# Attention masks of a two-layer graph network: transposed on TensorE, or by a casting DMA and a transposing DMA; with a sixth row buffer and a changed order of two small products

## The chip, the cores and the metric

The kernel runs on one core of a Trainium2 chip. The core has five engines, each with an instruction list of its own that it works through in order: TensorE (PE, with its weight loads shown apart as PEld), VectorE (DVE), ScalarE (ACT), GpSimd (POOL) and SyncE (SP). Engines wait for one another through semaphores. DMAs are issued here by SP and by POOL, in the order of those engines' lists. The metric is the time of one execution on the device in microseconds (us), the median of several runs; less is better.

## The reference, cut to what matters

The input x is 32 batches of 512 nodes with 256 features; adj is one 512 x 512 matrix of zeros and ones in int32 for each batch, about 3% of them ones. Two layers follow one another, and both read the same adj.

```
# layer 0
x = x + graph_conv(layernorm(x), adj)      # mean over neighbours, relu
x = x + ffn(layernorm(x))                  # tropical part and gated classical part

# layer 1, attention (4 heads of 64)
h      = einsum('bnd,hde->bhne', layernorm(x), W)
weight = leaky_relu(e_src[..., :, None] + e_dst[..., None, :])     # where adj == 1
weight = where(adj == 0, -1e9, weight)
att    = softmax(weight, axis=-1)
x      = x + layernorm_per_head(relu(att @ h + bias) + h)

# layer 1, mixer (8 heads of 64 slices)
sw = softmax((layernorm(x) @ W_x.T) @ W_slice.T / temp, axis=-1)   # nodes to 64 slices
st = sw.T @ fx / (sw.sum + 1e-5)                                   # slice tokens
ot = hydra(st)                # a scan over the 64 slice tokens, in both directions
x  = x + (sw @ ot) @ out_w.T + out_b
```

The attention types run from 1 to 5, but adj holds only 0 and 1, so one type counts. What the change touches is the mask `adj == 1` of the attention, which the kernel needs transposed: with the neighbour on the partitions and the node on the free axis.

## The kernel before, in words

**The two layers.** `layer0_sorted` does layer 0 for all batches. It sorts rows and gathers lines of a table, so it uses the DMA engines much. It ends at about 2324 us of the trace and leaves x in DRAM in a sorted order (`x2s`), with `ranks` saying where each row went. `layer1_plain` does layer 1. It is a generator: its constants and first preparations are woven into the last part of layer 0, up to its `yield True` at L1117. Both layers watch whether their shortcuts hold for the data; the findings are collected in `over`, and if any is set a plain version of both layers runs afterwards. With this input none is.

**Layer 1 by batch.** `attentions()` drives three generators a batch: `prepare(b)`, `attention(b)` and `norm(b)`.

- `prepare(b)` (L1156) gathers the batch's rows x on POOL with four indirect DMAs (L1162), normalises them (`normed`: statistics L1134 on VectorE, the power -0.5 at L30 and L31 on POOL, the scaling L1141 on ScalarE), adds a constant row by an accumulating DMA on POOL (`add_rows`, L949), and transposes the result (x3T, L1150 and L1151). It then forms h and both score vectors in one product (hp, L1188), their exponentials (L1191 to L1193) and a copy of h (ht, L1194). POOL adds a bias into hv (L1197); VectorE scales hv at L1210. The scores of the own node are transposed (minep, L1201), copied (L1203), written to DRAM by SP (ownd, L1205) and read back four times, once a head, as rows spread over all partitions (own, L1208). Tile own has 5 buffers.
- `attention(b)` (L1224) makes the weights of a head and of 128 neighbours in one VectorE instruction, att = max(own, other) * mask (`weigh`, L1221), 16 a batch. TensorE multiplies them with hv (avp, L1258) and sums them (adp, L1263).
- `norm(b)` (L1291 to L1313) adds ht, takes mean and mean square (the squares are written over ht at L1305, and reduced at L1307), and adds the normed values to x.

`mixer(g)` works on a group of GB = 2 batches: `slices` (layernorm, x4T, lgp L1344, exponentials sw L1345, the softmax over slices L1346 to L1351, yTp L1356, swp L1361), `tokens`, `scan` (the hydra part; `segp` L1500 are two products, one for each batch of the group, from the operands seg[0] and seg[1], and decay at L1502 is their exponential), and `unslice` (outp L1576, the addition to x L1578, the store of the result).

**The masks.** `masks(b)` is a generator that `prepare(b)` runs. For each of a batch's four tiles of 128 rows of adj it loads 256 KB of int32 (ai, L1087, issued by SP), turns it into bf16 on ScalarE (a, L1101), squares it on ScalarE (L1102), transposes its four blocks of 128 x 128 on TensorE into PSUM (maskp, L1092) and casts the result to uint8 on VectorE (mask, L1093; two buffers). ScalarE's two passes also leave row sums in `edges`. A sum of a that differs from the sum of its squares tells of values other than 0 and 1, and a sum of 0 of a node without a neighbour. Those become flags at L1610 to L1613. Batch 0's mask is made ahead, within layer 0.

**What sets the order.** Every tile name has a number of buffers, and an instruction that writes a buffer waits for the last reader of the one before. The program text is written in one order, by generators: `mixer` yields how many steps of preparation it wants, and the driver lets `attentions()` take them.

```python
PACE = 1.04 * GB * (TURNS + STEPS) / WANTED
for g in range(B // GB):
    for want in mixer(g):
        credit += want * PACE
        while credit >= 1.0:
            credit -= 1.0
            if next(ahead, True):
                credit = 0.0
```

STEPS counts the yields of a `prepare`. From this text a planner, with a cost for each instruction, fixes each engine's list before anything runs; a call within `keep_in_program_order` keeps its place in the text. A gather of batch b waits until the result of batch b - AHEAD_X is in the text (AHEAD_X = 5 buffers of x), so preparation runs at most so many batches ahead of `unslice`.

Of the kernel before, what the change touches and what calls it, by code (L numbers as in the profile page):

```python
# [864 lines left out]
def layer1_plain(tc, ident, eps, x2s, ranks, adj, w, out, over, ps):  # L865
# [21 lines left out]
    HE = HO + 1  # L887
    AP = AH // 2
    TURNS = AP * NT + 6
    STEPS = 15  # L890
    WANTED = 68
    AHEAD = 3
    ATT = 2 * (AHEAD + 2) + AP + 1
    HW = P // AH
    AHEAD_X = 2 * GB + 1
    PACE = 1.04 * GB * (TURNS + STEPS) / WANTED

    SMALL = 30.0 * 30.0 / D
# [2 lines left out]
    with ExitStack() as ctx:  # L901
# [3 lines left out]
        def ctile(name, shape):  # L905
            return cst.tile(shape, F32, tag=name, name=name)
# [8 lines left out]

        ones = ctile("ones", [P, P])
        nc.gpsimd.memset(ones, 1.0)
        identb = cst.tile([P, P], BF16, tag="identb", name="identb")
        nc.vector.tensor_copy(identb, ident)

        wa = ctile("wa", [P, DC, AH * HO + 2 * AH])
        for c in range(DC):
# [24 lines left out]
        def add_rows(xt, i):  # L947

            nc.gpsimd.dma_start(xt.rearrange("p t d -> p (t d)"), added[i].partition_broadcast(P), accum_op=ALU.add)  # L949

        yield
        edges = ctile("edges", [P, 2, B * NT])
        abias = const("abias", [P, AH * HO], w["gnn_bias"].rearrange("h e -> (h e)").partition_broadcast(P))
        gamma = const("gamma", [P, AH * HO], w["ln_gamma"].rearrange("h e -> (h e)").partition_broadcast(P))
        bfx = const("bfx", [P, KC, 1], w["b_fx"].rearrange("(k p o) -> p k o", p=P, o=1))
# [120 lines left out]
            nc.scalar.activation(ebsl, ebsl, AF.Exp)  # L1076

        se = ctx.enter_context(tc.tile_pool(name="e1", bufs=2, side="right", reuse_waits="tile"))
        masked = {}

        def masks(b, bank="any"):

            a, raw = [], []

            def load(t):
                raw.append(se.tile([P, N], I32, tag="ai", name=f"ai{b}_{t}", bufs=2))
                nc.sync.dma_start(raw[t], adj[b, t * P : (t + 1) * P, :])  # L1087

            def turn(t):
                pt = ps.tile([P, NT, P], BF16, tag=bank, name=f"maskp{b}_{t}")  # L1090
                for j in range(NT):
                    nc.tensor.transpose(pt[:, j, :], a[t][:, j * P : (j + 1) * P], identb)  # L1092
                nc.vector.tensor_copy(mask[:, :, t * P : (t + 1) * P], pt)  # L1093

            load(0)
            load(1)
            yield
            for t in range(NT):
                n = b * NT + t
                a.append(se.tile([P, N], BF16, tag="a", name=f"a{b}_{t}", bufs=3))  # L1100
                nc.scalar.activation(a[t], raw[t], AF.Identity, accum_out=edges[:, 0, n : n + 1])  # L1101
                nc.scalar.activation(raw[t], raw[t], AF.Square, accum_out=edges[:, 1, n : n + 1])  # L1102
                if t + 2 < NT:
                    load(t + 2)
                if t == 1:
                    mask = se.tile([P, NT, N], mybir.dt.uint8, tag="mask", name=f"mask{b}")
                    yield
                if t > 1:
                    turn(t - 2)
                    yield  # L1110
            for t in range(NT - 2, NT):
                turn(t)
                yield
            masked[b] = mask

        yield from masks(0, "mm")
        yield True  # L1117
        ps = ctx.enter_context(tc.tile_pool(name="p1", bufs=4, space=PSUM, reuse_waits="tile"))
        sb = ctx.enter_context(tc.tile_pool(name="s1", bufs=2, reuse_waits="tile"))
# [9 lines left out]
        def normed(xt, xn, name):  # L1129

            mv = sb.tile([P, NT, 2], F32, tag="mv" + name[0], name=f"mv{name}")
            for t in range(NT):
                st = sb.tile([P, 6], F32, tag="st" + name[0], name=f"st{name}_{t}", bufs=4)
                nc.vector.bn_stats(st, xt[:, t, :])  # L1134
                nc.vector.bn_aggr(mv[:, t, :], st)
            rs = sb.tile([P, NT], F32, tag="rs" + name[0], name=f"rs{name}")
            deviation(nc, rs, mv[:, :, 1], eps)
            shift = sb.tile([P, NT], F32, tag="shift" + name[0], name=f"shift{name}")
            nc.vector.scalar_tensor_tensor(shift, mv[:, :, 0], -1.0, rs, ALU.mult, ALU.mult)
            for t in range(NT):  # L1140
                nc.scalar.activation(xn[:, t, :], xt[:, t, :], AF.Identity, bias=shift[:, t : t + 1],  # L1141
                                     scale=rs[:, t : t + 1])
# [13 lines left out]
        def prepare(b):  # L1156

            while b >= AHEAD_X and b - AHEAD_X not in stored:
                yield True
            xt = xs[b] = sb.tile([P, NT, D], F32, tag="x", name=f"x{b}", bufs=AHEAD_X)  # L1160
            for t in range(NT):
                nc.gpsimd.indirect_dma_start(  # L1162
                    out=xt[:, t, :], out_offset=None, in_=x2s[b // SEG],
                    in_offset=bass.IndirectOffsetOnAxis(
                        ap=ranks[:, b * NT + t : b * NT + t + 1].bitcast(U32), axis=0))

            hv = sb.tile([P, NT, AH, HE], F32, tag="hv", name=f"hv{b}")
            xn = hv.rearrange("p t h e -> p (t h e)")[:, : NT * D].rearrange("p (t d) -> p t d", t=NT)
            edged = masks(b) if b not in masked else range(3)
            for i, _ in enumerate(edged):  # L1170
                if i < 3 or b not in masked:
                    yield
                if i == 2:
                    normed(xt, xn, f"c{b}")
                    add_rows(xt, 0)
                    yield
            mask = masked.pop(b)
            xnT = yield from turned(xn, "x3T", f"x3T{b}")
            yield


            ht = sb.tile([P, NT, AH * HO], F32, tag="ht", name=f"ht{b}")
            other = sb.tile([P, NT, AH], F32, tag="other", name=f"other{b}")
            mine = sb.tile([P, AH, NT], F32, tag="mine", name=f"mine{b}")
            for t in range(NT):
                ph = psum("any", f"hp{b}_{t}")
                for c in range(DC):
                    nc.tensor.matmul(ph[:, : AH * (HO + 2)], xnT[:, c, t * P : (t + 1) * P], wa[:, c, :],  # L1188
                                     start=c == 0, stop=c == DC - 1)
                d = ph[:, AH * HO : AH * HO + AH]  # L1190
                nc.scalar.activation(mine[:, :, t], ph[:, AH * (HO + 1) : AH * (HO + 2)], AF.Exp, scale=1.0 - SLOPE)  # L1191
                nc.scalar.activation(hv[:, t, :, HO], d, AF.Exp)
                nc.scalar.activation(other[:, t, :], d, AF.Exp, scale=SLOPE - 1.0)  # L1193
                nc.scalar.copy(ht[:, t, :], ph[:, : AH * HO])  # L1194
                yield

            nc.gpsimd.tensor_add(hv[:, :, :, :HO], ht.rearrange("p t (h e) -> p t h e", h=AH),  # L1197
                                 abias.rearrange("p (h e) -> p h e", h=AH).unsqueeze(1).to_broadcast([P, NT, AH, HO]))
            yield
            pt = psum("any", f"minep{b}")  # L1200
            nc.tensor.transpose(pt[: AH * NT, :P], mine.rearrange("p h t -> p (h t)"), ident)  # L1201
            row = sb.tile([AH * NT, P], F32, tag="turned", name=f"turned{b}", bufs=1)
            nc.scalar.copy(row, pt[: AH * NT, :P])  # L1203
            own_row = dr.tile([AH, N], F32, tag="own", name=f"ownd{b}")
            nc.sync.dma_start(own_row.rearrange("h (t p) -> (h t) p", p=P), row)  # L1205
            own = [wide("own", f"own{b}_{h}", AH + 1) for h in range(AH)]
            for h in range(AH):
                nc.sync.dma_start(own[h], own_row[h].partition_broadcast(P))  # L1208
            for t in range(NT):
                nc.vector.tensor_mul(hv[:, t, :, :HO], hv[:, t, :, :HO], hv[:, t, :, HO:].to_broadcast([P, AH, HO]))  # L1210
            ready[b] = mask, ht, hv, other, own
            yield
# [11 lines left out]
        def attention(b):  # L1224
# [52 lines left out]
            dt = back(dT, "dp")  # L1277
            rs = sb.tile([P, NT, AH], F32, tag="rs", name=f"rs{b}")
            nc.vector.tensor_scalar_max(rs, dt.rearrange("p (t h e) -> p t h e", t=NT, h=AH)[:, :, :, 0], 1e-30)
            nc.vector.reciprocal(rs, rs)  # L1280
            for q in range(AP):
                bt = back(vT[q], f"bp{q}_")
# [109 lines left out]
        def scan(g, uT):  # L1392
# [103 lines left out]
                    nc.tensor.matmul(pg[j * G : (j + 1) * G, i * G : (i + 1) * G], bcT[:, 0, j, :],  # L1496
                                     cpad[:, j, 2 * i : 2 * i + G], start=True, stop=True)
            pl = psum("any", f"segp{g}")
            for j in range(GB):
                nc.tensor.matmul(pl[j * G : (j + 1) * G, :], seg_l, seg[j], start=True, stop=True)  # L1500
            decay = inner(f"decay{g}")
            nc.scalar.activation(decay, pl, AF.Exp)  # L1502
# [104 lines left out]


        flags = over[:, 2 * AH + 3 :]
        nc.vector.tensor_sub(flags, edges[:, 1, :], edges[:, 0, :])  # L1610
        nc.vector.tensor_scalar(flags, flags, 0.0, None, ALU.not_equal)
        nc.vector.tensor_scalar(edges[:, 0, :], edges[:, 0, :], 0.5, None, ALU.is_lt)
        nc.vector.tensor_add(flags, flags, edges[:, 0, :])  # L1613


def layer1(tc, ident, eps, x2, adj, w, out):
# [632 lines left out]
```

## Time and profile before

| | |
|---|---|
| median of 3 runs | 4320.41 us (4319.69, 4320.41 and 4325.92) |
| the profiled execution | 4319.15 us |
| its span, first to last instruction | 4317.4 us |
| mean granted TensorE clock | 0.957 of full speed |
| busy: PE, PEld | 3852.3 us (89%), 2446.7 us (57%) |
| busy: DVE, ACT, POOL | 3233.1 us (75%), 2290.3 us (53%), 1540.2 us (36%) |
| moved by DMAs | 524.16 MB, 121 GB/s in the mean |
| 0 to 2200 us, mostly layer 0 | PE busy 1887 us, DMA engines 56% |
| 2324 to 2400 us, from layer 0 to layer 1 | PE busy 54 of 76 us |
| 2400 to 4180 us, layer 1 | PE busy 1683 us, DVE 1325, ACT 913, POOL 444, DMA engines 26% |

The page of the profile cuts the span into 40 equal slices and gives each engine's busy share in them in tenths. The groups of instructions name a line of the code, the engine, the operation, and what it writes and reads; then the busy time of all together, the mean of one in ns, and how long the engine stood idle just before them, with what ended the idle time. Waits are listed by the instruction that waited and the one that released it. The timeline lists single instructions with their start and their length in us, and in brackets the idle time before. SPq is SP's queue: the length there is the time to issue a DMA, not to carry it out; its landing is given apart.

### The profile page before, as it was taken

Reading aid. Unit: us, or ns where it says so; the run is one execution under the profiler, and the core shown is the slowest. Engines: PE = TensorE matmul, PEld = TensorE weight load, DVE = VectorE, ACT = ScalarE, POOL = GpSimd, SP = SyncE. Lnnn points to the kernel's source line nnn. Section 1 sums busy time; section 2 is a strip of 40 time slices with the busy share of each in tenths; the row PEclk is TensorE's granted clock in tenths of the full one; section 3 lists DMA queues with packets and bytes.
Section 4 is the critical chain, followed back from the end, with each engine's and each line's share of the span. In section 5 each row is a group of like instructions: output and inputs, shape, how many; then the busy total and the mean of one; then the engine's idle time right before and its main releaser. Section 6 shows DMA issues by size and latency. Waiting matters only on the chain.

```text
span 4317.4 us, 57903 instructions
## 1 busy us (share of the span) xinstructions
PE 3852.3 (89%) x20311; PEld 2446.7 (57%) x20311; DVE 3233.1 (75%) x7008; ACT 2290.3 (53%) x4756; POOL 1540.2 (36%) x1940
## 2 busy tenths in 40 slices
PE   5567998899999999889998899999999999999997
PEld 4454565566655665555555355565555555565555
DVE  6668877888788977877775777767777777778763
ACT  3344655556655656556664455545554455555432
POOL 2355643664435644354332222222222222222210
PEclk8678999999999999999999999999999999999998
DMA  4557654665546654386542322222222232222210
GB/s 130 161 160 228 191 162 133 192 214 168 149 127 218 197 165 136 109 279 192 153 128 69 78 67 71 79 62 67 74 69 69 76 79 76 75 69 74 62 30 16
DMA packets 260811, 524.16 MB, mean 121 GB/s; under 512 B 39800, under 2 KB 131588, under 8 KB 260509
## 3 DMA queue, kind: packets, MB, share of 16 engines
q0 software_dynamic: 124800, 366.28, 29.5%
q1 hardware_dynamic: 135708, 154.08, 11.4%
q8 instruction: 162, 2.65, 0.3%
q14 instruction: 141, 1.15, 0.1%
HBM read 463.11 MB, written 57.17 MB: 121 GB/s over the span
## 4 chain that ended last, share of the span: by engine, by line
PE 35%; DVE 26%; DMA 10%; issue 9%; POOL 8%; ACT 5%; SPq 0%; POOLq 0%; DVEq 0%; ACTq 0%
PE clsp L623 5%; DVE att L1221 4%; PE gatep L623 4%; PE po L652 3%; PE avp L1258 3%; DVE acc L637 3%; DMA rows<-table,xs 2%; PE yTp L1356 2%; DVE best L599 2%; DMA best<-table,xs 2%; DVE sw L1351 2%; DMA rows<-table,tops 2%; DVE sst L1349 2%; DVE sw L1346 2%; PE oTp L1544 1%
## 5 line engine op out<-in xcount | busy, mean ns | idle before, releaser
L623 PE MATMUL clsp<-xnT,wc 128*128 128x512 f32 x1024 | 522.4, 629 | 47.2 <-ACT cls L625 40.3
L623 PE MATMUL gatep<-xnT,wg 128*128 128x512 f32 x1024 | 496.8, 604 | 9.4 <-ACT gate L625 7.4
L652 PE MATMUL po<-wd,acc 128*128 128x256 f32 x2048 | 451.7, 380 | 5.2 <-DVE acc L641 4.3
L652 PEld LDWEIGHTS po<-wd,acc 128*128 128x128 f32 x2048 | 386.8, 190 | 70.7 <-issue 9.1
L1221 DVE SCALAR_TENSOR_TENSOR att<-own,other,mask 128x512 f32<-128x512 f32 x512 | 365.7, 743 | 78.5 <-DMA own<-ownd 78.5
L599 DVE SCALAR_TENSOR_TENSOR best<-rows,xs,best 128x1024 f32<-128x1024 f32 x212 | 271.0, 1280 | 132.6 <-ACT best L593 74.9
L637 DVE SCALAR_TENSOR_TENSOR acc<-past,fld,acc 128x512 f32<-128x512 f32 x448 | 332.1, 744 | 32.5 <-ACT past L636 24.3
L623 PEld LDWEIGHTS gatep<-xnT,wg 128*128 128x128 f32 x1024 | 196.1, 196 | 249.9 <-issue 198.4
L632 ACT ACTIVATE acc<-tz,fld 128x512 f32<-128x512 f32 x256 | 199.0, 777 | 260.1 <-PE tz L630 235.2
L636 ACT ACTIVATE past<-tz,fld 128x512 f32<-128x512 f32 x448 | 291.3, 693 | 73.3 <-DVE acc L637 72.7
L596 POOL DMA_INDIRECT rows<-table,xs x212 | 252.9, 1193 | 188.6 <-DVE best L599 124.8
L623 PEld LDWEIGHTS clsp<-xnT,wc 128*128 128x128 f32 x1024 | 183.7, 200 | 184.6 <-issue 113.3
L435 PE MATMUL pm<-h,adj 128*128 128x258 f32 (+1 forms) x1024 | 182.3, 325 | 98.5 <-DVE keep L428 35.7
L1258 PE MATMUL avp<-att,hv 128*32 128x512 f32 x2048 | 254.9, 603 | 13.9 <-DVE att L1221 13.8
L625 ACT ACTIVATE gate<-gatep,fld 128x512 f32<-128x512 f32 x256 | 175.5, 685 | 158.3 <-PE gatep L623 129.2
L1344 PE MATMUL lgp<-wsl,x4T 128*128 128x512 f32 x512 | 243.0, 613 | 16.6 <-ACT sw L1345 7.2
L1356 PE MATMUL yTp<-sw,x 128*128 128x512 f32 x512 | 237.8, 602 | 18.9 <-DVE sw L1351 18.2
L554 POOL DMA_INDIRECT xs<-rows_of,order x128 | 155.0, 1211 | 266.8 <-DVE acc L637 104.3
L1162 POOL DMA_INDIRECT x<-x2s,ranks x128 | 136.5, 1066 | 297.7 <-DVE att L1221 133.3
L1309 POOL TENSOR_TENSOR mu<-mu,eps 128x16 f32<-128x16 f32 x32 | 111.2, 3475 | 348.1 <-DVE mu L1308 347.9
L1576 PE MATMUL outp<-v,swT 128*128 128x256 f32 x1024 | 227.6, 381 | 0.0
L435 PEld LDWEIGHTS pm<-h,adj 128*128 128x128 f32 x1024 | 152.5, 214 | 123.9 <-issue 73.0
(590 smaller groups left out, 8643.8 us busy)
## 6 DMA issues: line engine op xcount, KB each, us to landing
adj<-in_adj POOLq DMA_DIRECT2D x128, 256.0 KB, 5.6
ai<-in_adj SPq DMA_DIRECT2D x128, 256.0 KB, 2.8
x<-added POOLq DMA_DIRECT2D x64, 512.0 KB, 5.2
own<-ownd SPq DMA_DIRECT2D x128, 256.0 KB, 3.6
rows_of<-keep SPq DMA_DIRECT2D x32, 550.0 KB, 4.3
x<-in_x SPq DMA_DIRECT2D x32, 512.0 KB, 6.6
xs<-bd POOLq DMA_DIRECT2D x32, 512.0 KB, 5.7
x2s<-xs SPq DMA_DIRECT2D x32, 512.0 KB, 3.0
```

Source lines behind the costliest of these rows:

```text
L435: nc.tensor.matmul(pm[:, : c1 - c0], a[:, i, t * P : (t + 1) * P], h[:, i, c0:c1], start=i + c0 == 0, stop=i + 1 == NT and c0 > 0)
L596: nc.gpsimd.indirect_dma_start(out=row, out_offset=None, in_=table, in_offset=bass.IndirectOffsetOnAxis(ap=idxs[:, k : k + 1].bitcast(U32) ...
L599: nc.vector.scalar_tensor_tensor(m, row, vals[:, k : k + 1], m, ALU.add, ALU.max)
L623: nc.tensor.matmul(pf, wf[:, c, f * P : (f + 1) * P], xnT[:, c, :], start=c == 0, stop=c == DC - 1)
L636: nc.scalar.activation(r, z, AF.Relu, bias=fld[:, f, AT + b : AT + b + 1])
L637: nc.vector.scalar_tensor_tensor(y, r, fld[:, f, CH + b : CH + b + 1], y, ALU.mult, ALU.add)
L652: nc.tensor.matmul(po[:, i, :], acc[f][:, t * P : (t + 1) * P], wd[:, f, :], start=f == 0, stop=f == FC - 1)
L1221: nc.vector.scalar_tensor_tensor(e, own[h], other[:, j, h : h + 1], mask[:, j, :], ALU.max, ALU.mult)
L1258: nc.tensor.matmul(pv[p][k * HW : (k + 1) * HW, :], hv[:, j, h, e : e + HW], weighed[b, h, j], **ends)
L1344: nc.tensor.matmul(pf, xnT[:, c, t * P : (t + 1) * P], wsl[:, c, :], start=c == 0, stop=c == DC - 1)
L1356: nc.tensor.matmul(py, xn[:, t, c * P : (c + 1) * P], sw[:, t, :], start=t == 0, stop=t == NT - 1)
L1576: nc.tensor.matmul(po[:, :D], swT[:, k, t * P : (t + 1) * P], v[:, k, :], start=k == 0, stop=k == KC - 1)
```

## The change

**Masks.** `masks()` goes, and with it the bf16 identity `identb`. Two small functions take its place. `shorten(b)` has POOL copy the whole adj[b] from DRAM to DRAM as bf16, one casting DMA (L1085 of the changed kernel; the tile short has three buffers, and the call keeps its place in the order of the text). `turn(b)` has SP load it with one transposing DMA of 512 KB into the mask (L1091), which is now bf16 with two buffers. Batches 0 and 1 are shortened ahead, within layer 0, and batch 0's mask is loaded there. `prepare(b)` starts by issuing turn(b) and shorten(b + 2), behind the row gathers. It yields the same number of times up to the normalisation as it did with a ready mask, so STEPS goes from 15 to 12.

**Watching the data.** One ScalarE pass over the whole mask, (mask - 0.5) squared, takes the place of two passes a tile. It writes into ht as scratch, before ht is made, and leaves a sum in `edges`; with zeros and ones alone the sum over a row of 2048 is 0.25 * 2048. Whether a node has a neighbour is now asked of the attention's denominator dt, a comparison of 128 x 4 values on VectorE. The flags at the end follow.

**A sixth buffer.** AHEAD_X goes from 5 to 6: x has six buffers, and a gather may come a batch earlier.

**decay's products.** The two products of segp are issued in the opposite order, seg[1] first, the operand that is made last.

```diff
-    STEPS = 15
+    STEPS = 12
-    AHEAD_X = 2 * GB + 1
+    AHEAD_X = 2 * GB + 2
...
-        identb = cst.tile([P, P], BF16, tag="identb", name="identb")
-        nc.vector.tensor_copy(identb, ident)
...
-        edges = ctile("edges", [P, 2, B * NT])
+        edges = ctile("edges", [P, B + B * NT])
+        centre = ctile("centre", [P, 1])
+        nc.gpsimd.memset(centre, -0.5)
...
-        def masks(b, bank="any"):
...
-        yield from masks(0, "mm")
+        short, masked = {}, {}
+        def shorten(b):
+            if b < B:
+                short[b] = dr.tile([N, N], BF16, tag="short", name=f"short{b}", bufs=3)
+                tc.keep_in_program_order(nc.gpsimd.dma_start(short[b], adj[b], max_dma_last_dim=8192))
+        def turn(b):
+            if b < B:
+                masked[b] = se.tile([P, NT, N], BF16, tag="mask", name=f"mask{b}")
+                nc.sync.dma_start_transpose(masked[b], short.pop(b))
+        for b in range(2):
+            shorten(b)
+            yield
+        turn(0)
         yield True
...
-            edged = masks(b) if b not in masked else range(3)
-            for i, _ in enumerate(edged):
-                if i < 3 or b not in masked:
-                    yield
-                if i == 2:
-                    normed(xt, xn, f"c{b}")
-                    add_rows(xt, 0)
-                    yield
+            if b:
+                turn(b)
+            shorten(b + 2)
+            yield
+            yield
+            yield
+            normed(xt, xn, f"c{b}")
+            add_rows(xt, 0)
+            yield
             mask = masked.pop(b)
...
             ht = sb.tile([P, NT, AH * HO], F32, tag="ht", name=f"ht{b}")
+            nc.scalar.activation(ht.rearrange("p t e -> p (t e)").bitcast(BF16), mask.rearrange("p t n -> p (t n)"),
+                                 AF.Square, bias=centre, accum_out=edges[:, b : b + 1])
...
+            nc.vector.tensor_scalar(edges[:, B + b * NT : B + (b + 1) * NT],
+                                    dt.rearrange("p (t e) -> p t e", t=NT)[:, :, 0], 0.0, None, ALU.is_le)
...
-            for j in range(GB):
+            for j in reversed(range(GB)):
                 nc.tensor.matmul(pl[j * G : (j + 1) * G, :], seg_l, seg[j], start=True, stop=True)
...
-        nc.vector.tensor_sub(flags, edges[:, 1, :], edges[:, 0, :])
-        nc.vector.tensor_scalar(flags, flags, 0.0, None, ALU.not_equal)
-        nc.vector.tensor_scalar(edges[:, 0, :], edges[:, 0, :], 0.5, None, ALU.is_lt)
-        nc.vector.tensor_add(flags, flags, edges[:, 0, :])
+        nc.vector.tensor_copy(flags, edges[:, B:])
+        nc.vector.scalar_tensor_tensor(flags[:, :B], edges[:, :B], 0.25 * NT * N, flags[:, :B],
+                                       ALU.not_equal, ALU.add)
```

More of the change, by code (lines that the diff above doesn't have):

```diff
@@ L1078, in layer1_plain @@
         se = ctx.enter_context(tc.tile_pool(name="e1", bufs=2, side="right", reuse_waits="tile"))
-        masked = {}
-        def masks(b, bank="any"):
[L1083 to L1096, printed above, removed]
-            yield
[L1098 to L1106, printed above, removed]
-                    yield
-                if t > 1:
-                    turn(t - 2)
-                    yield
[L1111 to L1114, printed above, removed]
-        yield from masks(0, "mm")
+        short, masked = {}, {}
[9 more added lines that the diff above has]
+            shorten(b)
+            yield
+        turn(0)
         yield True
@@ L1168, in prepare @@
             xn = hv.rearrange("p t h e -> p (t h e)")[:, : NT * D].rearrange("p (t d) -> p t d", t=NT)
-            edged = masks(b) if b not in masked else range(3)
-            for i, _ in enumerate(edged):
-                if i < 3 or b not in masked:
-                    yield
-                if i == 2:
-                    normed(xt, xn, f"c{b}")
-                    add_rows(xt, 0)
-                    yield
+            if b:
[7 more added lines that the diff above has]
+            yield
             mask = masked.pop(b)
```

## The prediction

> **What bounds the kernel now.** I read the page's time slices first, then the stretch table, the waits, the groups and the timeline. Each of the 40 slices is 108 us long; layer 1's first row gathers, at 2324 us, lie in the 22nd.
>
> ```profile
> PE   5567998899999999889998899999999999999997
> ...
> DVE  6668877888788977877775777767777777778763
> ACT  3344655556655656556664455545554455555432
> ...
> PEclk8678999999999999999999999999999999999998
> DMA  4557654665546654386542322222222232222210
> ```
>
> The last 17 slices are TensorE's: nine tenths or more, but for the last one, at full clock, with VectorE at seven to eight tenths and the DMA engines mostly at two. The stretch table (length; busy time and instructions of PE, weight load, VectorE, ScalarE, POOL; clock, DMA share, GB/s) gives this part in one row:
>
> ```profile
> 2400.00:4180.00 1780.00, 1683.19 (x11406) 1016.47 (x11399) 1324.54 (x2970) 912.66 (x2333) 444.14 (x404) 0.99 0.26 69
> ```
>
> TensorE is busy 1683 of 1780 us. The 97 us left are cut into short waits. The view of waits, from 2500 to 4180 us (who <- for whom: total us, times, longest us):
>
> ```profile
> PE yTp L1356 <- DVE sw L1351: 16.9, 21, 1.0
> PE oTp L1544 <- ACT yT L1538: 12.8, 15, 1.1
> PE maskp L1092 <- ACT sw L1345: 7.4, 6, 1.3
> ...
> PE maskp L1092 <- DVE mask L1093: 3.2, 4, 1.4
> ...
> PE avp L1258 <- DVE att L1221: 0.3, 1, 0.3
> ```
>
> No wait dominates, and the product that uses the masks waits 0.3 us in all. So a TensorE instruction removed here is worth its own time, and work taken from the others little. What the masks cost, from the groups of instructions (busy us, mean ns | idle before, and what ended it):
>
> ```profile
> L1093 DVE CAST mask<-maskp 128x512 uint8<-128x512 bf16 x128 | 85.8, 675 | 4.9 <-PE maskp L1092 4.6
> L1102 ACT ACTIVATE ai<-ai 128x512 int32<-128x512 int32 x128 | 81.9, 640 | 1.2
> L1101 ACT ACTIVATE a<-ai 128x512 bf16<-128x512 int32 x128 | 80.7, 631 | 96.8 <-PE maskp L1092 84.8 <-DMA ai<-in_adj 11.8
> ...
> L1092 PE MATMUL maskp<-identb,a 128*128 128x128 bf16 x512 | 46.1, 222 | 12.3 <-ACT sw L1345 7.4 <-DVE mask L1093 3.2 <-ACT a L1101 1.7
> ```
>
> The mean of 222 ns is a latency; pipelined, one takes 46.1/512 = 90 ns, and in the timeline a tile's four (a quartet) move the next product back by 0.22 to 0.43 us. By stretches the 46.1 us lie thus: 2.05 at 1969-2200, 2.46 at 2324-2400, 1.63 at 2400-2500, 38.37 at 2500-4060, 1.54 at 4060-4180.
>
> **What the Trainium skill says.** "DMA: Bandwidth & Descriptors", section "Issuing engines are not separate DMA queues": the DMAs of SP and POOL share the same 16 engines. The trace of before doesn't contradict it. A transposing load can therefore delay a load issued after it. "VectorE: DVE Perf Modes", section "The three transpose paths", says that PSUM is where a TensorE transpose ends and SBUF where a DMA one does: the trace shows the first half, the 128 casts out of PSUM. No run here shows a transposing DMA yet.
>
> **The change, part by part.**
>
> *Removed.* (1) 512 transposes on TensorE. Those in stretches that TensorE fills: 2.05 + 1.63 + 38.37 + 1.54 = 43.6 us, taken whole. The 2.46 us at 2324-2400 lie in a stretch where TensorE is busy 53.6 of 76 us: nothing. (2) Two ScalarE passes a tile: L1101 and L1102 (80.7 + 81.9 us) with their accumulator reads (25.2 and 26.2 us) are 214 us of ScalarE; 128 casts are 85.8 us of VectorE. TensorE hides both, except where they stand in a chain that it waits for. Its waits before the transposes go (7.4 + 3.2 = 10.6), but the PSUM bank waited for is then wanted by the next product: half, 5. And the casts stand between softmax steps (one starts at 3043.76 and one at 3046.97 us, beside the last scaling of sw), so I take 5 of the 16.9 us for yTp. Together -10; the ends are 0 and -48, half of all idle. (3) 128 loads of 256 KB on SP, hidden before too.
>
> *Added on POOL.* 32 casting DMAs, DRAM to DRAM. The nearest rows are the casting loads of layer 0 (adj, 626 ns to issue, 5.6 us to land for a quarter of a batch) and the accumulating DMA (931 ns): 32 x 0.63 to 0.93 = 20 to 30 us on an engine busy 444 of 1780 us. A batch's mask is cast two batches, some 117 us, before SP needs it; four times 5.6 us fits many times. Behind each in POOL's order stand row gathers, the rsqrt powers and the addition of hv. In steady state the gathers have slack, more with the sixth buffer. Once they haven't: after layer 0 three casts come among the first gathers, ahead of the first hv, while TensorE is starved: 3 x 0.93 = +3 us.
>
> *Added on SP.* 32 transposing DMAs of 512 KB. This is the unknown. Call its time from issue to landing T. Prices: "DMA: Bandwidth & Descriptors", section "Latency and other measured facts", gives 261 GB/s for the strided case, an estimate of 2.0 us; "The three transpose paths" gives 1309 ns for 128x128 in bf16, and sixteen of them in turn would be an estimated 20.9 us. I take 10 us. What T may be is read from the timeline; start and length of VectorE's last att of one batch, SP's write and VectorE's first att of the next (6.72 us is its wait), and TensorE's product that uses it:
>
> ```profile
> 2984.45 0.74 DVE L1221 SCALAR_TENSOR_TENSOR att<-own,other,mask 128x512 f32<-128x512 f32 x1
> ...
> 3004.32 0.33 SPq L1205 DMA_DIRECT2D ownd<-turned  x1
> ...
> 3010.72 0.75 DVE L1221 SCALAR_TENSOR_TENSOR att<-own,other,mask 128x512 f32<-128x512 f32 x1 [6.72 <-DMA own<-ownd]
> ...
> 3024.17 1.92 PE L1258 MATMUL avp<-att,hv 128*32 128x512 f32 x16
> ```
>
> In the changed program SP's transposition for batch b+1 stands ahead of ownd and the four own loads of b; it waits for the last att of b-1, which frees its buffer (2985.2), and ownd comes 19 us later. The next att then has 3024.2 - 3010.7 = 13.5 us before TensorE needs it. So T up to about 32 us is hidden behind TensorE's other products; beyond, each batch loses the excess. At 2, 10 or 21 us it costs 0.
>
> *Added on ScalarE.* One Square of 128x2048 a batch. L1305 takes 1048 ns for 1024 columns; "ScalarE: Activation LUTs", section "What ACT_TABLE_LOAD costs", gives about 1990 ns for 2048. 32 x 1.99 = 64 us against 214 removed. It adds waits: for the mask, and for the reduction that last read its ht buffer. Queued behind it is once a copy of x4T, which lgp needs; the mask is some 37 us old by then. The reduction may hold it 0 to 2 us a batch; with a copy of x4T already done ahead of it, I take 0.
>
> *VectorE.* A mask in bf16 for uint8 leaves att at 743 ns: L637, with three f32 operands, takes 744. The comparison of 128x4 adds 32 x 0.15 = 5 us, and the flags at the end a few tenths. Hidden; the 85.8 us removed are more.
>
> *Sixth buffer.* A gather is allowed one batch earlier. VectorE waits 47.9 us for gathers (stc), but TensorE hardly for what follows (hp <- x3T 1.7): 0, or -10 if the earlier start takes more from the chain. STEPS falls with the yields, 15 to 12, so the pace per batch stays.
>
> *decay's order.* The first product now waits for seg 1, made 0.6 us after seg 0. The second product waited for it before: seg 1 ends at 2987.23, the products begin at 2986.94, a loss of 0.3 us; 16 x 0.3 = 4.8 at most, 0 where both are long made. I take +2.
>
> Sum: -43.6 - 10 + 3 + 2 = -48.6 us. The profiled execution took 4319.15 us (span 4317.4 and 1.75 around it): 4270.6. The runs' median is 1.3 us higher; I forecast 4271, its own range 4240 to 4298.
>
> **Rivals.**
> *Deeper gain.* Where VectorE and ScalarE are lighter, the waits shrink too: half of 97 us, 4319 - 43.6 - 48 + 5 = 4232. For it: nearly all the waits are on these two. Against it: oTp <- yT is a pure chain of one copy.
> *Transposes were filler.* TensorE then waits where they stood, as at 3038.31, when a quartet is followed by 0.33 us for sw anyway. The time stays within 0.2% (what a measurement of this kernel can tell from no change), 4319. Against: most quartets have a product ready behind them.
> *The transposition holds up SP (slower).* With T over 32 us own and then att are late, at 30 batches x (T - 32). It cancels the gain from T = 32 + 48.6/30 = 33.6 us; at T = 36 it gives 4319 - 49 + 120 = 4390. For it: all in one queue, and own is already VectorE's longest wait (78.5 us). Against it: both prices lie below.
> *The change doesn't do what it says*, if the mask is still waited for because its buffer frees late: that is the same wait with a smaller T, and only in the first batches, where no mixer runs; some 10 us, 4281.
>
> **How the numbers follow.** Forecast 0.66 (with the late first masks), deeper gain 0.14, filler 0.07, late own 0.08, and 0.05 for a slower order of the list for no single cause. Faster 0.80, same 0.07, slower 0.13. The range reaches from below the deeper gain, 4225, to 4320, and leaves out most of the slower cases and a little below: 0.17.
>
> **What would show it.** Right: no maskp, TensorE's busy time 46 us lower, idle at 2400-4130 near 87 us; own's landing still about 4 us; transpositions landing in under 20 us. Wrong: avp waiting for att by more than 10 us in all, ScalarE waiting for mask DMAs, T above 30 us, or yTp's and lgp's waits grown by what the transposes gave up.

## The result, and the profile after

The changed kernel takes 4293.94 us (median of 6 runs, 4283.43 to 4311.61), the kernel before in the same comparison 4325.39 us (4319.69 to 4336.23): ratio 0.9928, 95% interval 0.9903 to 0.9952. That is 31 us less, where the forecast was 49 less (4271); the range of 4225 to 4320 holds it. On another chip the ratio was 0.9941 (0.9925 to 0.9957). The experiments show that the sum was nearer than its terms: the masks alone, which I had taken for the whole gain, make the kernel slower, and the sixth buffer, which I had costed at nothing, turns that into a gain. That the time fell into the range is therefore in part luck.

The time slices of the changed kernel (tenths busy, in 40 slices, as before):

```profile
PE   5567998989989999888999799999999999999997
DVE  6668887898778987777776677767777776777763
ACT  3344655566555665555665344454444444444533
PEclk8778999999999999998999899999999999999998
DMA  4547654575445754377552432333233333232210
```

Layer 1 looks as it did: TensorE at nine tenths, ScalarE and VectorE a little lighter, the DMA engines a little fuller. The profiled execution of this kernel took 4311.61 us; in it layer 0's last product came 19 us later than in the profile before. I don't count that as the change's: in three profiles with the old masks that product came at 2327.6, 2335.5 and 2340.9 us, and in a second profile of the changed kernel at 2332.1; and 16 of the 19 us had come by 1934 us of the trace, before the first cast was issued at 1962. So stretches of layer 1 are compared, from one product of decay to the next (one group of two batches).

Those stretches, from the second group's decay to the fifteenth's (thirteen groups), in the view of stretches: of the kernel before, and of the changed kernel in its second profile. The columns are the stretch, its length, busy time and instructions of PE, weight load, VectorE, ScalarE and POOL, clock, DMA share, GB/s.

```profile
2628.40:4163.90 1535.50, 1469.05 (x9961) 894.47 (x9958) 1138.85 (x2574) 791.30 (x2032) 391.75 (x359) 1.00 0.27 71
```

```profile
2639.30:4146.70 1507.40, 1437.89 (x9538) 868.87 (x9537) 1083.79 (x2479) 710.86 (x1685) 411.24 (x374) 0.99 0.30 70
```

By group the length falls from 118.1 to 116.0 us. TensorE's busy time falls by 2.4 us, VectorE's by 4.2 and ScalarE's by 6.2; TensorE's idle time rises from 5.1 to 5.3. The transposes are gone, but the waits that I expected to shrink by 10 us in all did not. From layer 0's last product to the first product of decay, the fill of layer 1, it is 181.4 us before and 190 after; from there to the end of the span it is 1808 before and 1777 after. So the groups give 32 us back and the fill takes 8, which is -23. The medians show -31 here and -26 on the other chip, and a profile is one execution.

TensorE's waits of the changed kernel, 2500 to 4180 us (total, times, longest):

```profile
PE yTp L1341 <- DVE sw L1336: 22.6, 17, 2.3
PE yp L1511 <- DVE mix L1504: 13.1, 14, 4.7
PE oTp L1529 <- ACT yT L1523: 9.4, 15, 0.7
PE yTp L1521 <- DVE y L1516: 8.9, 15, 1.7
PE yTp L1341 <- DVE sst L1335: 8.6, 6, 1.4
...
PE lgp L1329 <- ACT x4T L1131: 5.4, 2, 2.7
```

The wait of yTp for the softmax is 31.2 us over both rows, 16.9 before. Products of the scan wait longer too: yp 13.1 us (7.1 before), yTp at L1521 8.9 (1.5), vp 5.2 (not in the list before). Against that the 10.6 us at the transposes are gone with them, lgp no longer waits for x (6.7 before), and oTp waits 9.4 (12.8). Two groups of instructions, and the transposing DMA at its line (count, then issue time in ns, least, median and most):

```profile
L1241 PE MATMUL avp<-att,hv 128*32 128x512 f32 x2048 | 257.3, 605 | 30.8 <-DVE att L1204 30.8
L1164 ACT ACTIVATE ht<-mask,centre 128x2048 bf16<-128x2048 bf16 x32 | 64.1, 2002 | 84.3 <-DVE mu L1292 62.5 <-DMA x2s<-xs 17.1 <-issue 4.6
```

```profile
L1091 SPq DMA_TRANSPOSE mask<-short x32: 1719/2088/12447, 1991.8 to 4034.7; - x32
```

No instruction waits for a mask in steady state. The waits of avp for att, 30.8 us, all fall in the fill, before 2490 us (13.4 us there before), where VectorE's statistics of later batches stand ahead of att and wait for row gathers (17.3 us there, 5.1 before).

### The profile page after: what moved, and what is told of

Read it like the earlier page. It is cut to its first block, busy times and chain, and to the rows that moved or that the text cites. A ratio compares the mean times of both kernels' runs of the same rounds, so it can differ in the third digit from the quotient of the medians.

```text
span 4309.8 us, 56063 instructions
## 1 busy us (share of the span) xinstructions
PE 3825.7 (89%) x19799; PEld 2426.9 (56%) x19799; DVE 3170.3 (74%) x6909; ACT 2188.1 (51%) x4308; POOL 1584.8 (37%) x1973
## 2 busy tenths in 40 slices
DMA packets 313536, 524.04 MB, mean 122 GB/s; under 512 B 104823, under 2 KB 196611, under 8 KB 313244
## 4 chain that ended last, share of the span: by engine, by line
PE 43%; DVE 21%; DMA 10%; issue 8%; POOL 6%; ACT 4%; DVEq 0%; SPq 0%; POOLq 0%; ACTq 0%
PE clsp L623 5%; PE gatep L623 5%; PE po L652 5%; PE yTp L1341 4%; PE avp L1241 3%; DVE att L1204 3%; PE lgp L1329 3%; DVE acc L637 2%; DMA rows<-table,xs 2%; DVE best L599 2%; DMA best<-table,xs 2%; PE adp L1246 2%; DMA x<-x2s,ranks 1%; PE xp L1394 1%; PE hp L1171 1%
## 5 line engine op out<-in xcount | busy, mean ns | idle before, releaser
L1241 PE MATMUL avp<-att,hv 128*32 128x512 f32 x2048 | 257.3, 605 | 30.8 <-DVE att L1204 30.8
L1142 POOL DMA_INDIRECT x<-x2s,ranks x128 | 151.0, 1179 | 309.7 <-DVE x L1563 138.1
L1329 PE MATMUL lgp<-wsl,x4T 128*128 128x512 f32 x512 | 244.9, 620 | 13.1 <-ACT x4T L1131 7.2
```

What stands on the lines that cost most here:

```text
L1241: nc.tensor.matmul(pv[p][k * HW : (k + 1) * HW, :], hv[:, j, h, e : e + HW], weighed[b, h, j], **ends)
L1329: nc.tensor.matmul(pf, xnT[:, c, t * P : (t + 1) * P], wsl[:, c, :], start=c == 0, stop=c == DC - 1)
```

## The experiments

Each ratio is to the kernel before on the same chip (with its 95% interval):

| kernel | masks by DMA | row buffers | decay order | ratio |
|---|---|---|---|---|
| full change | yes | 6 | new | 0.9928 (0.9903 to 0.9952), 0.9941 (0.9925 to 0.9957) |
| masks alone | yes | 5 | old | 1.0042 (1.0025 to 1.0059) |
| decay's order alone | no | 5 | new | 1.0017 (1.0010 to 1.0024) |
| full, five buffers | yes | 5 | new | 1.0058 (1.0042 to 1.0075) |
| sixth buffer, with a shorter ring of attention tiles | no | 6 | old | 1.0037 (1.0024 to 1.0050) |
| full, old decay order | yes | 6 | old | 0.9918 (0.9903 to 0.9933), 0.9926 (0.9913 to 0.9939) |

**The parts one by one.** The masks' new path alone:

```diff
-    AHEAD_X = 2 * GB + 2
+    AHEAD_X = 2 * GB + 1
...
-            for j in reversed(range(GB)):
+            for j in range(GB):
```

> The kernel after with five row buffers and the old order of decay's products: only the masks' new path is left of the change. Theory of the prediction: the masks are the whole gain, so about 30 us below the kernel before (ratio 0.993), as the full change. Rival (the sixth buffer carries a good part, because earlier gathers leave VectorE less to wait for): about 15 us below (0.9965).

Measured: ratio 1.0042 (1.0025 to 1.0059), 18 us slower than before. Neither theory: the masks by DMA with five buffers are a loss.

The order of decay's products alone, in the kernel before:

```diff
-            for j in range(GB):
+            for j in reversed(range(GB)):
                 nc.tensor.matmul(pl[j * G : (j + 1) * G, :], seg_l, seg[j], start=True, stop=True)
```

> The kernel before with the two products of decay in the opposite order, nothing else. Theory: 0 to 5 us slower (1.000 to 1.001), since the first product waits for the operand made last. Rival (the new order gives the first product's group no second wait): up to 5 us faster, 0.999.

Measured: 1.0017 (1.0010 to 1.0024), 7 us slower. The sign is as I had it; the size is above my most of 4.8, to which the interval just reaches down. It isn't the wait that I priced: in this run's kernel the product of decay waits 0.2 us in all for its operand. With five buffers and the new masks the new order also stands 7 us above the old (4360.87 and 4353.67 us), but there the intervals overlap. What differs is the planned list: hp waits 11.5 us for the copies of x3T, 1.7 before. That this makes the 7 us is likely and not shown.

The full change with five buffers, and the full change beside it:

```diff
-    AHEAD_X = 2 * GB + 2
+    AHEAD_X = 2 * GB + 1
```

> The full change with five row buffers again, the order of decay's products new. Theory: as the full change, within 4 us. Rival: the sixth buffer moves gathers and their statistics ahead of the first attention after layer 0, as VectorE's waits for x in the changed profile suggest; then this is some 5 us faster than the full change; or it carries gain and this is 15 us slower.

> The changed kernel unaltered, on the same chip as the three others, as the number they are held against and for a second profile. The first profile showed layer 0 some 16 us slower before anything of the change had begun; if that was the execution and not the program, this profile's first row gathers start near 2327 us (2324 before), not at 2343. Expected ratio 0.993.

Measured: five buffers 1.0058 (1.0042 to 1.0075), six 0.9941 (0.9925 to 0.9957), in medians 4360.87 and 4305.62 us; in the second profile the row gathers start at 2328.7 us, so the late start of the first was that execution's. The sixth buffer is worth 55 us in the changed kernel. A group takes 119.7 us with five:

```profile
2647.10:4202.80 1555.70, 1454.44 (x9538) 873.90 (x9535) 1091.19 (x2488) 711.05 (x1685) 416.67 (x381) 0.98 0.31 69
```

Over thirteen groups that is 48 us more than with six: 32 us of TensorE's idle time, and 16.5 us of longer busy time for the same 9538 products.

**Where five buffers lose it.** POOL's wait for the store in that kernel, 2500 to 4180 us, and TensorE's for the softmax; then POOL's row in the kernel before:

```profile
POOL x L1142 <- DMA out<-x: 133.6, 17, 15.9
...
PE yTp L1341 <- DVE sw L1336: 61.7, 21, 6.5
```

```profile
POOL x L1162 <- DMA out<-x: 2.1, 2, 1.2
```

One place of it in the timeline, engine by engine (start, length, what, and the idle time before it with its releaser):

```profile
3638.63 0.61 POOL L1085 DMA_DIRECT2D short<-in_adj  x1
...
3648.36 1.06 POOL L1142 DMA_INDIRECT x<-x2s,ranks  x1 [5.28 <-DMA out<-x]
...
3650.72 2.93 POOL L1294 TENSOR_TENSOR mu<-mu,eps 128x16 f32<-128x16 f32 x1
```

```profile
3653.68 1.23 DVE L1297 TENSOR_TENSOR av<-av,mu 128x1024 f32<-128x1024 f32 x1 [8.53 <-POOL mu L1294]
...
3656.62 1.29 DVE L1331 TENSOR_TENSOR sw<-sw,ebsl 128x512 f32<-128x512 f32 x2
```

```profile
3660.08 8.40 PE L1341 MATMUL yTp<-sw,x 128*128 128x512 f32 x13 [6.45 <-DVE sw L1336]
```

The same gather in the kernel before, and the power of the norm behind it:

```profile
3033.24 1.02 POOL L1162 DMA_INDIRECT x<-x2s,ranks  x1 [0.19 <-issue]
...
3042.18 3.83 POOL L1309 TENSOR_TENSOR mu<-mu,eps 128x16 f32<-128x16 f32 x1 [2.64 <-DVE mu L1308]
```

These lines show a chain from a DMA over POOL and VectorE to TensorE. With five buffers the gather takes the buffer that the group just finished is storing, and waits for that store. The casting DMA was issued at 3638.63, one microsecond ahead of the store (SP's issue at 3639.80). The gather could start at 3648.36, 8.5 us after that issue; the gather for the store before it, with no cast just ahead, started 4.1 us after its issue (3629.52 and 3633.58). In the kernel before the store's median landing is 2.9 us. The norm's power mu stands behind the gather in POOL's list, VectorE's next step av behind mu, the softmax steps behind av in VectorE's list, and TensorE's yTp behind the softmax. In the kernel before the same gather stood ahead of the same power, and the store had landed.

The wait costs TensorE more than its length. Behind this one the granted clock was 0.51 from 3660 to 3665 us and 1.00 in the next 5 us, and all sixteen products of yTp took 9.69 us (the line above shows thirteen of them). At a clock of 1.00 twelve took 5.42 us in the changed kernel (shown further down), which is 7.2 for sixteen. Over thirteen groups yTp waits seven times for more than 5.4 us, and in the 5 us behind each of these waits the clock was 0.50 to 0.71. That fits the longer busy time; with six buffers the longest such wait is 2.4 us.

To see how much of it is the cast, the casts from batch 2 on were left out; the later batches then take the masks of batches 0 and 1 in turn:

```diff
+                if b > 1:
+                    short[b] = kept[b % 2]
+                    return
```

> The changed kernel with five row buffers, and without the casting DMAs from batch 2 on: the transposing DMA reads the bf16 copies of batches 0 and 1 in turn, so 30 casts are left out and later batches get the masks of the first two. Theory: the casting DMA lies beside the store of the result, the store lands late, the gather that waits for it holds POOL, and through the norm's power and VectorE's list TensorE waits at yTp; without the casts POOL's waits for the store (134 us) fall below 60 us, yTp's wait for sw from 62 to about 20 us, and the time to 4310 us or less, ratio 0.994. Rival (the order of POOL's list alone makes the wait, whatever the cast moves): within 10 us of the same kernel with casts, ratio 1.004 to 1.006.

Measured: 0.9993 (0.9978 to 1.0007), 28 us better than 1.0058, and not the 0.994 that I expected. POOL's waits for the store fall from 134 to 76 us (60 expected), yTp's from 62 to 44 (20 expected):

```profile
POOL x L1145 <- DMA out<-x: 76.2, 7, 14.9
```

So the casts, which move 1 MB in and 512 KB out each, are about half of the 55 us that five buffers lose. The timelines of the thirteen groups show which waits went. With the casts eight gathers wait 3.3 to 5.7 us for a store; without them the longest of these short waits is 2.4 us, and yTp's longest is 2.9, not 6.5. What stays are five waits of 14 to 15 us, in which POOL stands ready long before the store is issued (at 3633.58 14.68 us, of which 4.1 lie behind the issue); with six buffers three such waits stay too. Leaving out a cast takes away its transfer and its place in POOL's list together, and the run doesn't tell these apart; the late landing above speaks for the transfer. VectorE waits 65 us for the power, 91 with the casts, 50 with six buffers and 19 in the kernel before. The other half of the 55 us I did not isolate.

The sixth buffer in the kernel before, where it needed room that the ring of attention tiles gave up:

```diff
-    ATT = 2 * (AHEAD + 2) + AP + 1
+    ATT = 2 * (AHEAD + 2) + AP
-    AHEAD_X = 2 * GB + 1
+    AHEAD_X = 2 * GB + 2
```

> The kernel before, masks by TensorE as they were, with a sixth row buffer; to make room for it the ring of attention tiles has 12 buffers and not 13. Theory: in the kernel before a gather finds its buffer's store already landed (POOL waits 2.1 us in all for it), so the sixth buffer does nothing there: ratio 0.999 to 1.001. Rival (the sixth buffer is worth some 50 us whatever makes the masks, as it was between five and six buffers in the changed kernel): ratio near 0.988.

Measured: 1.0037 (1.0024 to 1.0050). The two edits together cost 16 us; which of them this run doesn't tell. With gathers allowed earlier POOL waits more for the store, 33 us over thirteen groups where it was 0.9. So a gain of 55 us from the sixth buffer is seen only beside the masks' new path; what it does by itself in the kernel before is not shown.

**The decay order inside the full change.**

```diff
-            for j in reversed(range(GB)):
+            for j in range(GB):
```

> The full change with decay's products in the old order. Theory: the new order costs here what it cost the kernel before and the changed one with five buffers, some 7 us; so this is 7 us below the full change (4305.6 on the last chip; ratio to the kernel before 0.9925 where the full change had 0.9941). Rival (the 7 us were a chance of the planner's list): as the full change.

> The full change with decay's products in the old order, once more, as the base of the two runs beside it. Theory: ratio 0.991 to 0.9935 again, so the first measurement (0.9918) stands.

Measured: 0.9918 (0.9903 to 0.9933), and again 0.9926 (0.9913 to 0.9939). The full change had 0.9928 and 0.9941. The means are some 5 us apart in the direction expected, but the intervals overlap, and a group takes the same time with both orders (116.0 and 115.8 us). Leaving the old order is the best kernel measured here; that it beats the full change is likely and not shown.

**What a transpose was worth.** 512 transposes of the mask, read by nobody, were put back where the old masks had them:

```diff
+        def fill(mask, b, t):
+            pt = ps.tile([P, NT, P], BF16, tag="any", name=f"maskp{b}_{t}")
+            for j in range(NT):
+                nc.tensor.transpose(pt[:, j, :], mask[:, t, j * P : (j + 1) * P], identb)
```

> The full change with the old order of decay's products, and 512 transposes of 128 x 128 put back on TensorE, 16 a batch in the places of the text where the old masks had them; they read the mask out of SBUF into PSUM, and nobody reads what they write. Theory of the prediction (a transpose removed is worth its own time): 43 us slower than its base, ratio near 1.002. Rival (the transposes filled waits that now show at yTp): at most 15 us slower, ratio 0.995. Between the two: the share of the transposes' time that was on the path.

Measured: 0.9984 (0.9976 to 0.9991), 25 us slower than the base beside it (4327.49 and 4302.70 us). The transposes' row, and the wait of yTp (22.7 us, and 8.7 more for sst, in the base):

```profile
L1098 PE MATMUL maskp<-identb,mask 128*128 128x128 bf16 x512 | 48.9, 224 | 5.6 <-ACT sw L1342 3.0 <-DMA mask<-short 2.0 <-DVE xs L654 0.6
```

```profile
PE yTp L1353 <- DVE sw L1348: 17.3, 14, 1.4
```

By group TensorE is busy 3.0 us more, idle 1.0 us less, and the group is 1.9 us longer. So about two thirds of a transpose's time in steady state was on the path, a third filled a wait. Besides yTp's wait, which falls from 31.4 to 17.3 us, yp's falls from 13.1 to 6.1. The timeline shows one such place. The kernel before, between the logits and yTp:

```profile
3036.15 0.39 PE L1092 MATMUL maskp<-identb,a 128*128 128x128 bf16 x4
3036.49 1.98 PE L1344 MATMUL lgp<-wsl,x4T 128*128 128x512 f32 x4
3038.31 0.39 PE L1092 MATMUL maskp<-identb,a 128*128 128x128 bf16 x4
...
3047.00 3.70 PE L1356 MATMUL yTp<-sw,x 128*128 128x512 f32 x8 [0.98 <-DVE sw L1351]
```

The changed kernel, the same batch, TensorE and then VectorE:

```profile
3045.87 1.88 PE L1329 MATMUL lgp<-wsl,x4T 128*128 128x512 f32 x4
...
3056.97 5.42 PE L1341 MATMUL yTp<-sw,x 128*128 128x512 f32 x12 [2.30 <-DVE sw L1336]
```

```profile
3053.57 1.32 DVE L1331 TENSOR_TENSOR sw<-sw,ebsl 128x512 f32<-128x512 f32 x2
3054.81 1.26 DVE L1334 TENSOR_REDUCE sst<-sw 128x8 f32<-128x512 f32 x2
3056.00 0.32 DVE L1335 RECIPROCAL sst<-sst 128x8 f32<-128x8 f32 x2
3056.23 1.28 DVE L1336 TENSOR_TENSOR sw<-sw,sst 128x512 f32<-128x512 f32 x2
```

From the first lgp of this batch to the second part of yTp it is 18.0 us before (3028.96 to 3047.00) and 16.8 after (3040.18 to 3056.97). TensorE's work there is not the same: three quartets went, and the planner put four products of hp and four more of x3T in and moved four of yTp behind the wait. Its idle time in the stretch grew from 1.3 to 3.0 us. VectorE has no gap there from the norm's steps to the last softmax step, in either kernel: in this stretch it is VectorE's list that TensorE waits for, in a kernel that TensorE bounds as a whole.

**Other places for the casts.** Behind the addition of hv's bias, and ahead within layer 0; both with the old decay order:

```diff
             if b:
                 turn(b)
-            shorten(b + 2)
...
+            shorten(b + 2)
             yield
             pt = psum("any", f"minep{b}")
```

> The full change with the old order of decay's products and with each cast issued behind the addition of hv's bias, not behind the row gathers: it no longer lies beside the store of the result, nor among the first gathers after layer 0. Theory: the waits for the store shrink also with six buffers, and the transition gains 3 to 5 us: 5 to 15 us below the same kernel with the cast in its old place. Rival: with six buffers the store's landing is off the path, no change.

Measured: 0.9978 (0.9965 to 0.9991), against 0.9918 of the same kernel with the cast in its old place: 28 us slower where 5 to 15 faster was expected. POOL's waits for the store did fall, from 72 to 34 us over thirteen groups, and yTp's rose from 29 to 36. The store was then not what the group waited for. A group is 1.1 us longer. One thing that grew is VectorE's wait at att for the own rows, from 51 to 72 us over thirteen groups: the cast now stands ahead of SP's write and reads of these rows. Whether that makes the loss is not shown.

```diff
-        for b in range(2):
+        for b in range(5):
             shorten(b)
...
-            shorten(b + 2)
+            if b > 1:
+                shorten(b + 3)
```

> The full change with the old order of decay's products, and with the casts of batches 0 to 4 issued within layer 0 (the DRAM tile has six buffers); prepare of batch 2 goes on with batch 5. No cast stands among the first gathers after layer 0. Theory: the fill of layer 1 (from layer 0's last product to the first product of decay, 189 us with the casts, 185 in the run without casts, 181 before) falls to about 185, and the time by 4 us against its base. Rival: the casts cost layer 0 as much as they save here, no change.

Measured: 0.9920 (0.9905 to 0.9934), the base 0.9926: no difference, and the fill stays at 190 us. So the casts among the first gathers are not what makes the fill 8 us longer. The avp of the first batches still waits 28 us for att (31 in the base, 13 before) and VectorE's statistics 15 us for gathers (19 and 5). The cause of the longer fill is open.

**The two DMAs by themselves.** Six casts, and six transposing DMAs each with a reader, behind the last batch:

> The full change with the old order of decay's products, and behind the last batch six rounds of one cast, one transposing DMA and one small VectorE copy that waits for it; nothing else runs then. It measures the two DMAs by themselves. The prediction took 10 us for the transposing DMA from issue to landing, with 2.0 and 20.9 us as the two ends; a cast of 1 MB to 512 KB at the rate of layer 0's casting loads (256 KB in 5.6 us) would take up to 22 us, at the accumulating DMA's 5.2 us for 512 KB as little as 5 us.

VectorE's readers in the timeline, with their waits; SP issued the six transposing DMAs at 4300.57, 4304.37, 4308.25, 4311.40, 4314.63 and 4316.8 us:

```profile
4308.07 0.15 DVE L1600 CAST seen<-pmask 128x1 f32<-128x1 bf16 x1 [7.51 <-DMA pmask<-probe]
4311.22 0.15 DVE L1600 CAST seen<-pmask 128x1 f32<-128x1 bf16 x1 [3.00 <-DMA pmask<-probe]
4312.90 0.15 DVE L1600 CAST seen<-pmask 128x1 f32<-128x1 bf16 x1 [1.52 <-DMA pmask<-probe]
4315.75 0.15 DVE L1600 CAST seen<-pmask 128x1 f32<-128x1 bf16 x1 [2.70 <-DMA pmask<-probe]
```

From the start of its issue to its reader a transposition takes 7.5, 6.9, 4.7, 4.4, 4.4 and 4.6 us; 10 were taken in the forecast. The casts' landings show only in sum: from their issue (4282.6 to 4285.7 us) the DMA engines stood at nine tenths or more for about 20 us. That is at most 3.3 us of all 16 engines for each, since two stores of 512 KB were issued in that time. The transposing DMAs fill the engines as well: seven tenths or more from 4304 to 4320 us. So one of them could hold up a store as a cast does; no run tests that.

## Why the prediction was right, and where not

**Right: bound, sign and removal.** TensorE bounds layer 1 (95% of the stretch is its busy time), the transposes went, and TensorE's busy time fell by 2.4 to 2.6 us a group, about 40 us over 16 groups against the 43.6 of the sum. No product waits for a mask in steady state.

**The number was in part luck.** The forecast took its gain from the masks and nothing from the sixth buffer. By that reckoning the masks with five buffers had to gain about 50 us; they lose 18. The time came back into the range through a part of the change whose worth I had not seen. Two of the signs that I had set down for being wrong did appear: avp waits for att by more than 10 us (31, all in the fill), and yTp's wait grew (16.9 to 31.2; lgp's did not).

**Right: the transposing DMA is hidden.** 4.4 to 7.5 us behind the last batch, where the timeline allowed 32. This rests on the probe and on the absence of waits for the mask. The rival of a slow transposition falls. What I wrote for it was not right: own is not VectorE's longest wait in the kernel before (78.5 us); hv waits 173.8 us for POOL.

**Wrong term: the waits, -10.** They came out at some +4 us (0.25 a group). "A TensorE instruction removed here is worth its own time" was too strong, and "the transposes were filler" too, as a whole: transposes put back cost 25 us, of 49 busy. The sentence that VectorE's casts of the mask stood between softmax steps pointed at the right place; what I didn't do was to see whether VectorE had gaps there without the casts. It has none.

**Wrong step: "Sixth buffer ... 0, or -10".** The run with five buffers is 55 us slower than with six, and with five the change is a loss. I had asked what an earlier gather brings, and answered from the kernel before, where gathers have slack. I should have asked what a later store takes, once something new shares its way.

**Wrong step: the casts on POOL.** I priced their issue (0.61 us measured, 0.63 taken) and what stands behind them in POOL's list, and found slack in when SP needs the result. I left out what they do to a transfer beside them: the store of the result, for which POOL's next gather waits, with the norm's power behind it. My search for late work went by the consumer of the cast, not by its neighbours on the DMA engines. With six buffers VectorE still waits 50 us over thirteen groups for that power, 19 before.

**Mis-sized: the transition, +3.** It is +8, and not for the reason given: casts moved out of it change nothing.

**Mis-sized: decay's order, +2.** 7 us when made alone, and not by the product's own wait (0.2 us); the planned list differs. In the full change it lies between 0 and 10, not separated.

**Square.** It takes 2.00 us, as the price said, and waits 62.5 us in all for the reduction that last read its buffer. lgp waits 5.4 us for a copy of x4T queued behind it, in two groups; 0 was taken.

In one sum, with the rates of the thirteen groups taken for all sixteen: -40 (TensorE) + 4 (waits) + 8 (fill) is -28; the runs show -31 on one chip and -26 on the other.

## What to carry to other kernels

Before a buffer is costed at nothing, follow what the transfer that frees it shares its way with after the change, and what stands behind the waiting instruction on its engine. Here a cast beside a store reached TensorE over POOL and VectorE. In a kernel bound by one engine as a whole, look for the stretches where another engine has no gap: work taken from the first is there worth only part of its time. A long wait of TensorE can cost more than its length, so look at the granted clock behind it. And parts of a change may not add up: the masks alone, decay's order alone, and the sixth buffer with the shorter ring were each slower than before, all together faster.

## What the runs showed of the hardware

SP needs 2.1 us (median) to issue a transposing DMA of 512 KB, where four plain loads of 256 KB (own) take 1.75 us together; the first one took 12.4 us, in layer 0 (8.2 in the second profile). It moves small packets: those under 512 bytes rise from 39800 to 104823 for 32 of them, some 2030 each; leaving out 30 casts takes only 480 away. Behind a wait of TensorE of 5.4 us or more the granted clock of the next 5 us was 0.50 to 0.71 in the kernel with five buffers, seven times of seven; behind one wait of 2.3 us with six buffers it was 0.72.
